# A macaron block with a state-space convolution: the convolution's rows turned by VectorE and gathered by DMA, the half chunk first in the last wave, and three bursts of small work cut into pieces

## The chip, the core and the metric

The kernel runs on one core of one Trainium2 chip. A core has TensorE (PE; its weight loads are listed apart as PEld), VectorE (DVE), ScalarE (ACT), GpSimd (POOL) and SyncE (SP), which here does nothing but issue DMAs, one after the other in the order of its queue. All five run their own instruction lists and meet at semaphores. The time is the device time of a whole launch in microseconds (us), the median of a few runs.

## The reference, cut to what matters

For 2048 rows of 1024 floats the block computes

```python
x = u                                            # (2, 1024, 1024) float32
x = x + 0.5 * ffn(layernorm(x))                  # silu(xn @ Wg) * (xn @ Wu) @ Wd, 4-bit weights
x = x + s4(layernorm(x))                         # causal convolution along the last axis, and D * u
x = x + 0.5 * ffn(layernorm(x))                  # the same weights again
```

Wg and Wu have shape (1024, 2752), Wd has (2752, 1024). A weight is `scales[g] * (w4 - (z4[g] + 1))` with one scale and zero point for each of 8 groups of 128 rows of Wg and Wu, and for each of 21.5 groups of Wd. The convolution in the middle runs along the 1024 columns of each row with one kernel K for all rows, so it is a product of the normalized rows with a Toeplitz matrix made from K.

## The kernel before, in words

**Jobs.** The 2048 rows are four blocks of 512 (`TB`), each four tiles of 128 rows (`t` = 0 to 3). A feed-forward pass over a block is a job. `JOBS` orders the eight: (block 0, first pass), (1, first), (0, second), (1, second), (2, first), (3, first), (2, second), (3, second). They are called job 0 to job 7 here. The work between two passes of a block (layer norm, convolution, layer norm) is hidden in the job that follows the block's first pass: block 0's in job 1, block 1's in job 2, block 2's in job 5, block 3's in job 6. These four are called the jobs with a convolution.

**Up and down.** `gate_up` runs 64 steps: 8 waves of column chunks, 8 groups of 128 contraction rows each. A chunk is 128 hidden columns, with a gate unit (even number) and an up unit (odd). The first five waves hold three chunks, that is six units, each in one PSUM bank of [128, 512]; the last three hold two, and the very last also the half chunk, unit 42, whose 64 gate and 64 up columns share a bank. In a step each unit gets two matmuls, one with the activations' low part `xTl` and one with the high part `xTh` (line 774). After each group the unit is multiplied in PSUM by a ratio of scales (`scaled`, lines 739 on ScalarE and 743 on VectorE), so that the unit's next matmul must wait for that. After the eighth group `gated` (lines 801, 804, 806, 808) makes the hidden chunk. `down` runs 44 steps in the same manner (line 849), four banks at a time. A step with six units has 12 matmuls, one with four 8, the last wave's 10.

**Weights.** For each step SP loads a tile of bytes (`load_bytes`, L700 and L707, six buffers) four steps ahead, and POOL casts it (L716, five buffers) three steps ahead. In job 0 the bytes are also made first: VectorE splits words (`split`, L590 to L594), POOL casts (L623), DMAs write and read them back.

**Order.** Side work is hung on steps: `at(up, s, f)` runs `f` when step `s` is written, at its middle for half numbers; `dn` is the same for `down`. A list scheduler then sets each engine's order; `in_order_of_writing` and `pinned` keep named engines in the order of the text. `in_pieces` lets a generator run one piece per step.

**The convolution before.** For each tile `norm` (`normalized`, L230) writes the normalized rows on VectorE, `swap` (`turn_whole`) has PE transpose them in eight 128x128 pieces into two PSUM banks (`turned`, L237), and ScalarE (L1260) and VectorE (L1258) copy a bank each to `st`. `convolve` then makes three sums on POOL (L1205, L1206 and the line after) and the products on PE (L1210) in two halves, which VectorE adds to `x` (L1240 to L1250). Counted in steps, with `late` = 33 in job 1 and 16 else, tile `t` is normalized at `late+8+4t`, turned at `late+10+4t` and multiplied at `late+12+4t`.

**Small work.** `scales_down` (one call at step 40 of job 0) turns the scales of Wd and makes their ratios in a handful of VectorE operations. `in_order` (one call at step 30 of job 2) checks on the chip that scales and group indices are as the fast way needs them; it ends with one matmul (L491) and a flag that is read at the very end.

**Buffers that the change shares.** `t4` tiles are [128, 1024] float32, ten buffers; `results_out` already turns the down product of each job with VectorE's 32x32 transposes (`turn_block`, L884) and sends it through DRAM (`rows_out`, L890: 32 partitions of 16 pieces of 512 bytes in one DMA).

Of the kernel before, what the change touches and what calls it, by code (L numbers as in the profile page):

```python
# [57 lines left out]
def macaron_s4_kernel(  # L58
# [320 lines left out]
    def inverse(inv, s, name):  # L379

        sq = t2(f"sq_{name}")[:, : s.shape[1]]
        nc.vector.tensor_tensor(sq, s, s, ALU.mult)
        nc.vector.scalar_tensor_tensor(inv, sq, 2.0**-60, s, ALU.is_lt, ALU.add)
        nc.vector.reciprocal(inv, inv)
# [47 lines left out]
    def scales_down(rows):  # L432
        ps = bank("ps_d")
        for i, row in enumerate(rows):
            for k in range(4):
                nc.tensor.transpose(
                    ps[:, bass.ts(4 * i + k, GD)], row[:GD, bass.ts(k, P)], ident[:GD, :GD]
                )
        n = NC * GD
        flat = s_dn.rearrange("p c g -> p (c g)")  # L440
        nc.vector.tensor_copy(flat, ps[:, :n])
        inv = t2("inv_d")[:, :n]
        inverse(inv, flat, "d")
# [3 lines left out]
        )  # L447
        nc.vector.tensor_scalar(
# [3 lines left out]
    def in_range(s, col):  # L452

        n = s.shape[1]
        sq = t2(f"rs_{col}")[:, :n]
        nc.vector.tensor_tensor(sq, s, s, ALU.mult)
        for k, (op, lim) in enumerate(((ALU.is_ge, 2.0**-60), (ALU.is_le, 2.0**60))):
            t = t2(f"rg_{col}_{k}")[:, :n]
            nc.vector.tensor_scalar(t, sq, lim, None, op)
            nc.vector.tensor_reduce(ok[:, col + k : col + k + 1], t, AX.X, ALU.min)  # L460

    def in_order():

        nc.gpsimd.memset(ok, 1.0)
        in_range(s_gu.rearrange("p u g -> p (u g)"), 0)
        in_range(s_dn.rearrange("p c g -> p (c g)"), 2)
# [11 lines left out]
        f = t4("ixf")[:32, : 3 * P].rearrange("p (i k) -> p i k", i=3)  # L478
        nc.vector.tensor_copy(f, raw)
        nc.vector.tensor_scalar(f, f, float(GD - 1), None, ALU.min)  # L480
        want = small.tile([32, 1], F32, tag="want", name="want")
        nc.vector.tensor_scalar(want, row_t[:32], float(GD - 1), None, ALU.min)
        nc.vector.tensor_scalar(f, f, want, None, ALU.is_equal)
        nc.vector.tensor_reduce(
            ok[:GK, 4:5], f[:GK, 0:2].rearrange("p i k -> p (i k)"), AX.X, ALU.min
        )
        nc.vector.tensor_reduce(ok[: full + 1, 5:6], f[: full + 1, 2], AX.X, ALU.min)
        all_ok = small.tile([P, 1], F32, tag="all_ok", name="all_ok")
        nc.vector.tensor_reduce(all_ok, ok[:, 0:6], AX.X, ALU.min)
        ps = bank("ps_ok")  # L490
        nc.tensor.matmul(ps[:1, :1], all_ok, ok[:, 6:7], start=True, stop=True)  # L491
        nc.vector.tensor_scalar(flag, ps[:1, :1], P - 0.5, None, ALU.is_lt)
# [252 lines left out]
    def gate_up(j, b, hooks):  # L745
        hi, lo = pieces[b]
        ps = {}
        for s, (wi, g) in enumerate(STEPS):
# [6 lines left out]
            if wi == len(WAVES) - 1:  # L755
                order.append((2 * WIDE, 2 * n))


            early = len(order) // 2
# [1085 lines left out]
```

## Time and profile before

| | us |
|---|---|
| median of 3 runs | 2079.88 (2078.57 to 2081.78) |
| the profiled execution, whole | 2081.12 |
| its span | 2079.2 |
| PE busy in the span | 2031.7 |
| DVE busy | 1670.2 |
| ACT busy | 1398.8 |
| POOL busy | 1352.6 |
| PE busy from 1571 to 1755 (up part of job 6, with a convolution) | 183.67 of 184 |
| PE busy from 1834 to 1989 (up part of job 7, without) | 155.00 of 155 |

The profiled execution took 1.92 us more than its span and 1.24 us more than the median. Busy times are unions, so overlapping matmuls count once. The granted clock of TensorE was 0.995 on average.

### The profile page before, as it was taken

How to read it: one execution, taken by the hardware profiler on the slowest of the kernel's cores; microseconds unless marked ns; L12 is line 12 of the kernel's file. 1: busy time of each engine (PE TensorE's matmuls, PEld its weight loads, DVE VectorE, ACT ScalarE, POOL GpSimd, SP SyncE). 2: the span in 40 equal slices, each digit the busy share in tenths (PEclk: the TensorE clock that was granted, in tenths of full speed). 3: DMA queues.
4: the chain of work that ended last, by engine and by line, in shares of the span. 5: the costliest groups of instructions: out<-in, count | busy, mean ns of one | idle time of the engine just before them, and what ended most of it. 6: DMA issues, size and time to landing. Idle time of an engine off the chain costs nothing.

```text
span 2079.2 us, 30011 instructions
## 1 busy us (share of the span) xinstructions
PE 2031.7 (98%) x9332; PEld 1388.2 (67%) x9332; DVE 1670.2 (80%) x2813; ACT 1398.8 (67%) x2185; POOL 1352.6 (65%) x1740
## 2 busy tenths in 40 slices
PE   6999999999999999999999999999999999999998
PEld 4555675676866768665776568667686676866576
DVE  8888878778789787797788877787877878777777
ACT  6677787645775477677777777664776647767775
POOL 5766668655875468755876568654696546975542
PEclk9999999999999999999999999999999999999999
DMA  4334323112621116511472116311164111661113
GB/s 143 118 91 143 109 82 83 35 55 51 164 81 40 51 45 158 177 34 35 105 177 95 32 43 156 101 40 48 36 152 113 40 48 33 149 183 50 34 35 101
DMA packets 278023, 180.38 MB, mean 87 GB/s; under 512 B 101253, under 2 KB 257774, under 8 KB 277854
## 3 DMA queue, kind: packets, MB, share of 16 engines
q1 hardware_dynamic: 276550, 175.96, 30.8%
q8 instruction: 76, 1.25, 0.3%
q10 hardware_dynamic: 1016, 1.82, 0.2%
q14 instruction: 93, 0.76, 0.1%
q0 software_dynamic: 288, 0.59, 0.1%
HBM read 119.13 MB, written 40.18 MB: 77 GB/s over the span
## 4 chain that ended last, share of the span: by engine, by line
PE 89%; DVE 6%; POOL 2%; DMA 1%; issue 1%; ACT 1%; SPq 0%; ACTq 0%; POOLq 0%; DVEq 0%
PE pg L774 55%; PE po L849 29%; PE pc L1210 3%; DVE pg L743 1%; PE pb L1210 1%; DMA b<-wq 1%; DVE po L743 1%; PE st L237 1%; DVE x L263 0%; POOL q L623 0%; DMA x<-in_L_attn_u_dram 0%; DVE hf L804 0%; POOL w_up L716 0%; DMA wq<-q 0%; DVE xn L230 0%
## 5 line engine op out<-in xcount | busy, mean ns | idle before, releaser
L739 ACT ACTIVATE pg<-pg,rat 128x512 f32<-128x512 f32 x1240 | 787.1, 660 | 418.2 <-PE pg L774 415.9
L743 DVE TENSOR_TENSOR pg<-pg,rat 128x512 f32<-128x512 f32 x1168 | 775.3, 692 | 162.3 <-PE pg L774 154.2
L774 PE MATMUL pg<-xTh,w_up 128*128 128x512 f32 x2752 | 851.4, 437 | 2.4 <-DVE pg L743 1.8
L774 PE MATMUL pg<-xTl,w_up 128*128 128x512 f16 x2752 | 717.6, 383 | 12.8 <-DVE pg L743 6.9
L716 POOL CAST w_up<-b 128x768 fp32r<-128x768 int8 (+2 forms) x490 | 375.4, 772 | 429.6 <-PE pg L774 323.0
L774 PEld LDWEIGHTS pg<-xTh,w_up 128*128 128x128 f32 x2752 | 520.6, 189 | 178.7 <-issue 14.3
L739 ACT ACTIVATE po<-po,ratd 128x512 f32<-128x512 f32 x660 | 432.0, 661 | 159.6 <-PE po L849 158.8
L849 PE MATMUL po<-hl,w_down 128*128 128x512 f32 x1344 | 528.8, 396 | 6.1 <-DVE po L743 5.3
L849 PE MATMUL po<-hh,w_down 128*128 128x512 f32 x1344 | 520.9, 391 | 0.0
L743 DVE TENSOR_TENSOR po<-po,ratd 128x512 f32<-128x512 f32 x620 | 429.1, 695 | 110.5 <-PE po L849 108.7
L774 PEld LDWEIGHTS <-w_up 128*128 128x128 bf16 x2752 | 226.6, 99 | 338.5 <-issue 159.5
L716 POOL CAST w_down<-bd 128x512 fp32r<-128x512 int8 x352 | 217.1, 620 | 149.7 <-PE po L849 87.8
L849 PEld LDWEIGHTS po<-hl,w_down 128*128 128x128 f32 x1344 | 251.7, 188 | 76.9 <-DVE po L743 15.6
L849 PEld LDWEIGHTS po<-hh,w_down 128*128 128x128 f32 x1344 | 253.0, 188 | 50.2
L808 POOL TENSOR_TENSOR hl<-hf,hh 128x512 fp32r<-128x512 f32 x168 | 219.4, 1306 | 8.0
L804 DVE SCALAR_TENSOR_TENSOR hf<-pg,rat,g 128x512 f32<-128x512 f32 x168 | 123.5, 747 | 42.3 <-ACT g L801 33.3
L806 POOL CAST hh<-hf 128x512 fp32r<-128x512 f32 x168 | 106.4, 634 | 65.8 <-DVE hf L804 33.0
L801 ACT ACTIVATE g<-pg,rat 128x512 f32<-128x512 f32 x168 | 110.8, 686 | 41.0 <-PE pg L774 26.2
L900 POOL TENSOR_TENSOR x<-x,yr 128x512 f32<-128x512 f32 x52 | 66.7, 1284 | 0.0
L289 POOL TENSOR_TENSOR lo<-x,hi 128x512 f16<-128x512 f32 x48 | 61.8, 1288 | 0.0
L189 DVE BATCH_NORM_STATS2 stats<-x 128x6 f32<-128x512 f32 x88 | 60.1, 682 | 0.0
L287 POOL TENSOR_TENSOR mid<-hi,top 128x512 bf16<-128x512 f32 x48 | 56.0, 1167 | 0.0
(219 smaller groups left out, 1106.0 us busy)
## 6 DMA issues: line engine op xcount, KB each, us to landing
b<-wq SPq DMA_DIRECT2D x319, 96.0 KB
bd<-wdq SPq DMA_DIRECT2D x336, 64.0 KB
x<-in_L_attn_u_dram SPq DMA_DIRECT2D x30, 512.0 KB
yz<-y SPq DMA_DIRECT2D x56, 256.0 KB
yr<-yz SPq DMA_DIRECT2D x56, 256.0 KB
b<-wq SPq DMA_DIRECT2D x128, 64.0 KB
xs<-x SPq DMA_DIRECT2D x16, 512.0 KB
x<-xs SPq DMA_DIRECT2D x16, 512.0 KB
```

The lines of the kernel that those rows point to most:

```text
L289: nc.gpsimd.tensor_tensor(lo[:, own], n[:, own], hi[:, own].bitcast(F32), ALU.subtract)
L716: nc.gpsimd.tensor_copy(t, b)
L739: nc.scalar.activation(dst, src, AF.Copy, scale=sc)
L743: nc.vector.tensor_tensor(dst, src, sc.to_broadcast(list(dst.shape)), ALU.mult)
L774: nc.tensor.matmul(p, weights, (lo, hi)[k][:, g, :], start=(g == 0 and not done), stop=(g == GK - 1 and done), skip_group_check=True,)
L801: nc.scalar.activation(g, pg, AF.Silu, scale=rat[:, 2 * f, GK - 1 :])
L804: nc.vector.scalar_tensor_tensor(hf, pu, last, g, ALU.mult, ALU.mult)
L806: nc.gpsimd.tensor_copy(hi, hf)
L808: nc.gpsimd.tensor_tensor(lo, hf, hi.bitcast(F32), ALU.subtract)
L849: nc.tensor.matmul(ps[c], w[:, bass.ts(c, P)], part, start=(f == 0 and k == 0), stop=(f == NF - 1), skip_group_check=True,)
L900: nc.gpsimd.tensor_tensor(part, part, rows_back.pop((a, t)), ALU.add)
L1210: nc.tensor.matmul(dst, lhsT, rhs, start=start, stop=stop, skip_group_check=True)
```

## The change

The normalized rows of a tile are no longer turned by PE. `rows_turned` normalizes them in two halves and then transposes 32x32 blocks in place, 256 columns at a time, six VectorE pieces on six half steps. `rows_stored` writes the tile to a DRAM tile (two of them, used in turn), and `columns_loaded` reads it back with four DMAs, one for each 32 partitions of `st`, 32x32 pieces of 32 floats (128 bytes) each, which completes the transposition. With `start_` = 36 and `gap` = 3.5 in job 1, 23 and 4 else, tile `t` starts at o = `start_ + gap*t`; the pieces lie at o to o+2.5, the store at o+4, the four loads at o+7, the product's halves at o+10 and o+11. The layer norms around it move with it.

The half chunk comes first instead of last in the last wave, and is now in its early group. In job 1 ScalarE takes every other scaling of each wave's first up unit for the whole job, not only up to step 32. `scales_down` is given in pieces from step 40 to 51.5, `in_order` in pieces over steps 36 to 59 of job 3, not at once in job 2. Some layer-norm pieces of other jobs move.

```diff
-    def inverse(inv, s, name):
+    def inverse_in_pieces(inv, s, name):
         sq = t2(f"sq_{name}")[:, : s.shape[1]]
         nc.vector.tensor_tensor(sq, s, s, ALU.mult)
+        yield
         nc.vector.scalar_tensor_tensor(inv, sq, 2.0**-60, s, ALU.is_lt, ALU.add)
+        yield
         nc.vector.reciprocal(inv, inv)
...
             if wi == len(WAVES) - 1:
-                order.append((2 * WIDE, 2 * n))
-            early = len(order) // 2
+                order.insert(0, (2 * WIDE, 2 * n))
+            early = (len(order) + 1) // 2
...
-                    if pos == 1:
-                        on_act = (j == 0 and g % 4 == 0) or (j == 1 and s < 32 and g % 2 == 0)
+                    if unit == 2 * fs[0] + 1:
+                        on_act = (j == 0 and g % 4 == 0) or (j == 1 and g % 2 == 0)
...
+    s_dram = [dpool.tile([P, HID], F32, tag=f"sz{i}", name=f"sz{i}") for i in range(2)]
...
-                    late, first = (33, 27) if j == 1 else (16, 15)
+                    first, start_, gap = (26, 36, 3.5) if j == 1 else (13, 23, 4)
...
-                    steps = [(up, late + 4 + i) for i in range(4)]
+                    steps = [(up, start_ + i - 4 if j != 1 else start_ - 2 + i / 2) for i in range(4)]
                     in_pieces(at, steps, lambda: deviations_in_pieces(pb, 2))
-                    def norm(t):
-                        s4n[t] = normalized(pb, t)
-                    def swap(t):
-                        s4x[t] = turn_whole(s4n.pop(t), f"st_{pb}_{t}")
+                    def rows_turned(t):
+                        m, r, _ = ln[pb, t]
+                        n = s4n[t] = t4(f"xn_{pb}_2_{t}")
+                        for half in range(2):
+                            own = bass.ts(half, 512)
+                            nc.vector.tensor_scalar(n[:, own], x[pb][t][:, own], m, r, ALU.subtract, ALU.mult)
+                            yield
+                        for i in range(4):
+                            own = n[:, bass.ts(i, 256)]
+                            nc.vector.transpose(own, own)
+                            yield
+                    def rows_stored(t):
+                        nc.sync.dma_start(s_dram[t % 2], s4n.pop(t))
+                    def columns_loaded(t):
+                        s4x[t] = s = t4(f"st_{pb}_{t}").rearrange("p (c t) -> p c t", c=NC)
+                        src = s_dram[t % 2].rearrange("(b i) (c a j) -> a i c b j", i=Q, a=NQ, j=Q)
+                        for q in range(NQ):
+                            dst = s[bass.ts(q, Q)].rearrange("p c (b j) -> p c b j", j=Q)
+                            nc.sync.dma_start(dst, src[q])
...
-                        at(up, late + 8 + 4 * t, lambda t=t: norm(t))
-                        at(up, late + 10 + 4 * t, lambda t=t: swap(t))
-                        at(up, late + 12 + 4 * t, lambda t=t: conv(t))
-                        at(up, late + 13 + 4 * t, lambda t=t: next(parts[t], None))
-                    steps = [(up, late + 15 + 4 * t + i) for t in range(NT) for i in range(2)]
+                        o = start_ + gap * t
+                        steps = [(up, o + i / 2) for i in range(6)]
+                        in_pieces(at, steps, lambda t=t: rows_turned(t))
+                        at(up, o + 4, pinned(lambda t=t: rows_stored(t), ET.SP))
+                        at(up, o + 7, pinned(lambda t=t: columns_loaded(t), ET.SP))
+                        at(up, o + 10, lambda t=t: conv(t))
+                        at(up, o + 11, lambda t=t: next(parts[t], None))
+                    steps = [(up, start_ + gap * t + 13 + i) for t in range(NT) for i in range(2)]
                     in_pieces(at, steps, lambda: moments_by_tile(pb, 3, halves=True))
...
-                at(up, 40, lambda: scales_down(rows.pop("down")))
+                steps = [(up, 40)] + [(up, 41.5 + 2 * i) for i in range(6)]
+                in_pieces(at, steps, lambda: scales_down(rows.pop("down")))
...
-            if j == 2:
-                at(up, 30, in_order)
+            if j == 3:
+                in_pieces(at, [(up, 36 + i) for i in range(24)], in_order)
...
-                        steps = [(up, s) for s in range(18, 27)]
+                        steps = [(up, s) for s in range(12, 21)]
                         in_pieces(at, steps, lambda: moments_by_tile(ab, 1, halves=True))
-                        steps = [(up, s) for s in range(28, 32)]
+                        steps = [(up, s) for s in range(21, 25)]
...
-                        d, where = ((23 + 4 * t + 2 * half, dn), (3 * t + half, dn))[min(j, 1)]
+                        d, where = (23 + 4 * t + 2 * half if j == 0 else (0.5, 6, 14, 20)[t] + half), dn
                         if j > 1:
-                            d, where = (50 if ak == 3 else 33) + 2 * t + half, up
+                            d, where = (54 if ak == 3 else 25) + 2 * t + half, up
```

## The prediction

> **What bounds the kernel now.** I read the page's busy times and chain first, then the stretches of the jobs, then PE's order of time where the change works, then VectorE's and SP's rows.
>
> ```profile
> PE 2031.7 (98%) x9332; PEld 1388.2 (67%) x9332; DVE 1670.2 (80%) x2813; ACT 1398.8 (67%) x2185; POOL 1352.6 (65%) x1740
> PE 89%; DVE 6%; POOL 2%; DMA 1%; issue 1%; ACT 1%; SPq 0%; ACTq 0%; POOLq 0%; DVEq 0%
> ...
> 1571.00:1755.00 184.00, 183.67 (x911) 120.66 (x911) 150.45 (x266) 112.65 (x177) 102.17 (x123) 1.00 0.18 53
> 1834.00:1989.00 155.00, 155.00 (x688) 93.26 (x688) 117.53 (x180) 110.23 (x173) 91.48 (x111) 1.00 0.25 75
> ```
>
> PE is busy 98% of the span and is 89% of the chain that ends last. The two stretches (columns: length, then busy time and count of PE, PEld, DVE, ACT, POOL, granted clock, DMA share, GB/s) are the up parts of job 6, with a convolution, and job 7, without: PE never stops in either, so the convolution's 29 us are PE's own work. What leaves PE there leaves the time, as long as nothing else comes to hold it up.
>
> PE's order of time (start, length, operation) shows what leaves:
>
> ```profile
> 1640.78 0.82 PE L774 MATMUL pg<-xTl,w_up 128*128 128x512 f16 x3
> 1641.44 1.04 PE L237 MATMUL st<-ident,xn 128*128 128x128 f32 x8
> 1642.31 0.81 PE L774 MATMUL pg<-xTl,w_up 128*128 128x512 f16 x3
> ```
>
> The next matmul starts 0.87 us after the first transpose, so a tile's eight transposes cost 0.87 us; the 1.04 overlaps.
>
> The other losses are a few waits in jobs 0, 1, 2 and 5 (in brackets: idle time before, and who ended it), and what follows two of them:
>
> ```profile
> 155.97 0.38 PE L774 MATMUL pg<-xTl,w_up 128*128 128x512 f16 x1 [2.14 <-DVE pg L743]
> 494.49 0.79 PE L849 MATMUL po<-hl,w_down 128*128 128x512 f32 x1 [1.95 <-DVE po L743]
> 672.86 0.19 PE L491 MATMUL ps_ok<-ok,all_ok 128*1 128x1 f32 x2 [0.46 <-DVE all_ok L489]
> ...
> 156.00:165.00 9.00, 8.70 (x30) 3.94 (x29) 7.37 (x12) 5.19 (x9) 4.20 (x6) 0.81 0.67 213
> 490.00:500.00 10.00, 7.72 (x25) 5.23 (x25) 9.31 (x13) 4.18 (x7) 8.63 (x12) 0.83 0.08 22
> ```
>
> After each 2 us wait the granted clock falls: 0.81 over 9 us and 0.83 over 10 us are both about 3.4 us at half speed (9 x 0.19 x 2; 10 x 0.17 x 2), which costs 1.7 us more.
>
> **The change, part by part.**
>
> *Transposes off PE.* Four jobs x 4 tiles x 0.87 = **-14.0 us**. The built order of the changed kernel has these 128 matmuls gone, so this part is real if nothing new stops PE. Sixteen ACT copies (585 ns) go too; ACT is at 67% and gains nothing by it.
>
> *VectorE's share.* Rows that price it (minimum/median/maximum in ns):
>
> ```profile
> L263 DVE TENSOR_SCALAR x<-x,mv,r x56: 528/539/1539, 253.7 to 1740.1; 128x512 f32<-128x512 f32 x56
> L230 DVE TENSOR_SCALAR xn<-x,mv,r x16: 793/803/1865, 414.1 to 1678.1; 128x1024 f32<-128x1024 f32 x16
> L884 DVE STREAM_TRANSPOSE y<-y x112: 402/433/436, 296.5 to 2038.7; 128x256 f32<-128x256 f32 x112
> L1258 DVE COPY st<-st x16: 676/682/692, 419.7 to 1696.2; 128x512 f32<-128x512 f32 x16
> ```
>
> Added per tile: 2 x 0.54 + 4 x 0.43 = 2.80 us. Removed: 0.80 + 0.68 = 1.48. Net +1.3 us, 5.3 us a job, in up parts where VectorE has 184 - 150 = 34 us free. Locally it is tight: an up step is 2.70 us (24 steps in 64.9 us at the start of job 6), VectorE scales three units of it at 0.63 us each when back to back (four took 2.52 us), and over the three steps of a tile's pieces it has 3 x 1.89 + 2.80 = 8.5 us to do in 8.1, with a free step behind. But this very load exists already: the down result's L884 transposes come two a step beside three scalings, and through them the chain is one unbroken PE piece:
>
> ```profile
> 838.18 107.63 PE pg L774 x479
> ```
>
> So I cost this at nothing in the forecast; the cover is the eight matmul slots (8 x 0.225 = 1.8 us) between a unit's last matmul of one step and its first of the next, of which the scaling takes 0.7. If the cover goes, the next scaling is late and PE waits in each tile (rival 1). Waits of 0.89 us in job 5 (at 1375 us) and 1.25 us in job 1 (at 415 to 425 us, for the st copies, sums and scalings) come from the long normalize and the copies that go: **-1.7**.
>
> *The way through DRAM.* The trace has no load in 128-byte pieces of this size. The nearest is the down result's store:
>
> ```profile
> L890 SPq DMA_DIRECT2D yz<-y x56: 318/721/1457, 306.2 to 2041.5; - x56
> SPq L700 <- POOL w_up L716: 761.4, 386, 6.8
> ```
>
> Four such DMAs in a row (at 848.5 us) hold SP 3.4 us, the last up to 1.46, and the byte load behind them 1.39 where 0.32 is its rule: once the queue is full, 512 pieces need 1.45 us, 2.8 ns a piece. By pieces a column load (1024) takes 2.9 us and a tile's four 11.6; by bytes (a load has half the 256 KB) 0.73 and 2.9. I take the pieces, the costlier. Behind the four on SP stand the byte loads of later steps. They have room: of SP's waits, 761 us are byte loads waiting for a free buffer. With 6 byte and 5 weight buffers load k may go when PE has done step k-11, and its cast may start when PE has done k-5, six steps or 16 us later; SP loses about 9 of them. Then the product: turned at o+2.5 steps (6.8 us), store landed about 3.5 us on, loads 11.6, landing 1.9 (the time to landing that the page has for POOL's stores): 23.8 us, against 27 us at step o+10. In job 1 the steps after 40 take 1.8 us; by the same sum its loads of tiles 1 and 2 are 1 to 2 us late. POOL's three sums wait in its queue, casts behind them, but casts run three steps ahead. I take **+2.5 us** for job 1 and jitter together (0 by bytes, up to 6).
>
> Here the Trainium skill speaks against the change: "DMA: Bandwidth & Descriptors", Rules for kernel authors, wants a turning DMA to be the hardware's transpose and not a rearranged pattern, and puts 19x between them. The trace's DMA transposes of a 256 KB tile hold SP 1.25 us (L294); two of them for float32, times 19, would be 47 us a tile, 30 more than the 17 us (four steps and a product of 6.2) that a tile has, and 16 x 30 us on the sum. I follow L890: pieces of 128 bytes are no single elements, and a scattered store at 2.8 ns a piece is in this trace.
>
> *scales_down in pieces.* The 2.14 us wait in job 0 stands between its operations of 1.18, 1.39 and 1.19 us (L382, L383, L384), bunched with `split`. Spread over 12 steps, each meets the slack alone. Worth 2.14 plus 1.7 of clock. By the skill ("TensorE: Matmul & The Clock Gate", table of goals) only idle gaps over about 3 us lower the clock, so by the rule 2.1; the trace has the fall after 2.14 and 1.95, and I go by it: up to 3.8. Some may return as a wait for the weights that job 0 is making, so **-3.0** (0 to -3.9).
>
> *Half chunk first, job 1's scalings and layer norm.* At job 0's end PE waits 1.35 us for a scaling behind the half chunk's split on VectorE (L823, L825); the half chunk now ends six matmuls (1.35 us) sooner: **-0.7** (+0.5 to -1.5). At job 1's end there are waits of 0.33, 1.95, 0.55 and 0.34 us behind deviations, L818 and L263, and 1.7 of clock, 4.9 together. The deviations now end half a step sooner, normalizing starts half a step later and is spread over 21 down steps, L818 comes sooner, and sixteen scalings of 0.69 us go to ACT. But the last product comes about a step later, so **-2.5** (+1 to -4.5).
>
> *The check.* Job 2's 0.46 wait and a 0.54 wait at 649 us among its L459 pieces go; in job 3 its pieces are single and its matmul stands a step behind its operand: **-0.9**. The other layer-norm pieces move within up parts where VectorE has a fifth free, and the block that they read is loaded from step 6: nothing.
>
> Sum: -14.0 - 1.7 + 2.5 - 3.0 - 0.7 - 2.5 - 0.9 = **-20.3**. From the profiled execution 2081.12 - 20.3 = 2060.8; that run stood 1.24 over the median, so the median becomes 2079.88 - 20.3 = **2059.6**.
>
> **The rivals.** *1, VectorE becomes the bound around the tiles.* For: 8.5 us in 8.1. L263 reaches 1.5 us where it meets other work. Against: the unbroken stretch at 838. At 0.6 us in each of 16 tiles, +10: 2070 (2066 to 2075).
>
> *2, the waits of jobs 0 and 1 only move.* For: VectorE is 85% busy there. Then -14.0 - 1.7 - 0.9 + 2.5 = -14.1: 2066.
>
> *3, slower: SP's queue is overrun by the column loads.* A tile has 17 us; other loads take about 2 of them. From (17 - 2)/4096 = 3.7 ns a piece lateness piles up from tile to tile, in the convolution jobs; all of the gain is gone at 20/16 = 1.25 us a tile, 4.0 ns. At 6 ns a tile needs 26.6, 9.6 too many; only the tiles after the first of each job are late, 12 x 9.6 = 115: about 2175. For: 2.8 is not far from 3.7, and the kind is not in the trace. Against: pieces carry a quarter of L890's bytes.
>
> That the change doesn't do what it says is excluded for the transposes by the built order.
>
> **How the numbers follow.** The forecast 0.68 (2053 to 2066), rival 1 0.16, rival 2 0.07, rival 3 0.06, something between that ends at no change 0.03. Faster by over 0.2% (4.2 us, about what a measurement can tell): 0.68 + 0.16 + 0.07 = 0.91; within 0.2%: 0.03; slower: 0.06. The range reaches from all gains at their bounds (2053.5) into rival 1 (2070.5).
>
> **What would show it.** Right: L237 keeps only job 0's 32 transposes; job 6's up part is about 180.5 us with PE busy throughout; the clock stays at 1.00 at 150 to 165 and at 480 to 500 us; 128-byte DMAs hold SP under 3 us. Wrong: PE waits before L1210 for a POOL sum or a DMA (rival 3), before L774 for L743 within the pieces of each tile (rival 1), or a clock of 0.8 again at either place (rival 2).

## The result, and the profile after

| | median, us | runs |
|---|---|---|
| before | 2080.83 | 2078.57 to 2082.32 |
| after | 2065.81 | 2064.28 to 2067.67 |

Each was timed four times here; before's first three are those of the table further up. The ratio is 0.9929, with a 95% interval from 0.9912 to 0.9946: 15.0 us faster (11 to 18). The forecast was 2059.6, in a range from 2053.5 to 2070.5. The profiled execution has a span of 2062.2 us where before had 2079.2.

The profile after, first the busy times and then the chain by engine:

```profile
PE 2011.6 (98%) x9204; PEld 1370.9 (66%) x9204; DVE 1666.7 (81%) x2861; ACT 1397.5 (68%) x2185; POOL 1349.8 (65%) x1740
PE 88%; DVE 4%; POOL 2%; DMA 2%; issue 1%; ACT 1%; SPq 0%; ACTq 0%; POOLq 0%; DVEq 0%
```

PE has 128 matmuls fewer and is busy for 20.1 us less: 14.0 are the transposes, and most of the rest is the clock, which fell in four windows fewer (further down). It still bounds everything. The stretches that answer to those of before (length, busy time and count of PE, PEld, DVE, ACT, POOL, granted clock, DMA share, GB/s): the up parts of job 6 and job 7, and the two places where the clock fell:

```profile
1557.00:1740.00 183.00, 180.96 (x881) 117.11 (x880) 152.08 (x281) 110.35 (x174) 100.04 (x123) 1.00 0.30 76
1818.00:1973.00 155.00, 155.00 (x690) 93.40 (x689) 118.00 (x180) 110.64 (x174) 91.43 (x111) 1.00 0.25 76
150.00:165.00 15.00, 14.48 (x63) 7.31 (x61) 13.20 (x23) 12.26 (x21) 10.44 (x12) 1.00 0.51 151
480.00:500.00 20.00, 19.31 (x82) 13.67 (x81) 17.46 (x32) 14.47 (x23) 16.09 (x22) 1.00 0.11 32
```

Both places have the full clock now. But job 6, where PE was without a gap before, has 2.04 us of gaps, and is only 1.3 us shorter (from its first matmul of up to its first of down, 183.1 instead of 184.4), although 3.5 us of transposes are gone. PE's list of waits (what waited, for what: total us, times, longest us) names the new one, and PE's order of time shows the first of the six (in brackets: idle before, and what ended it; `pc` and `pb` are the two PSUM banks of a tile's products):

```profile
PE pb L1232 <- POOL sums L1227: 5.7, 6, 1.7
```

```profile
653.35 1.47 PE L1232 MATMUL pc<-near,st 128*128 128x256 f32 x8
654.65 0.39 PE L1232 MATMUL pc<-after,st 128*128 128x128 f32 x2
654.88 0.39 PE L1232 MATMUL pc<-ahead,st 128*128 128x128 f32 x2
656.94 0.49 PE L1232 MATMUL pb<-near,sums 128*128 128x128 f32 x2 [1.68 <-POOL sums L1227]
```

The products from `st` run, so the columns are there; only the product from `sums` waits. POOL's order of time at that moment says why:

```profile
653.43 0.60 POOL L827 CAST hh<-hf 128x512 fp32r<-128x512 f32 x1
654.12 1.26 POOL L829 TENSOR_TENSOR hl<-hf,hh 128x512 fp32r<-128x512 f32 x1
655.33 0.61 POOL L827 CAST hh<-hf 128x512 fp32r<-128x512 f32 x1
655.90 0.99 POOL L1227 TENSOR_TENSOR sums<-st 128x384 f32<-128x384 f32 x1
```

The first sum, for which PE waits, stands behind the splitting of the wave's three hidden chunks (three `hh` and two `hl`), which comes at the end of each wave. The new steps put a tile's product at the second step of a wave (step 33), where this splitting is under way. PE waits 1.68 us for the first tile and 0.22 us for the third, in each of jobs 2, 5 and 6.

The DMA that finishes the turning is cheap (count, then minimum/median/maximum ns on SP):

```profile
L1564 SPq DMA_DIRECT2D st<-sz x64: 562/675/1885, 407.3 to 1679.5; - x64
L1553 DVE STREAM_TRANSPOSE xn<-xn x64: 390/432/445, 399.5 to 1669.3; 128x256 f32<-128x256 f32 x64
```

1024 pieces of 128 bytes hold SP 0.68 us, and no product waits for `st`. VectorE's part did no harm in these jobs: in job 5 PE is one piece of the chain through the steps in which the rows of the first tiles are turned.

```profile
1295.06 86.47 PE pg L795 x384
```

Taken apart by job (time from the first matmul of one job to that of the next, less the same in before; the last column is the span):

| us | job 0 | 1 | 2 | 3 | 4 | 5 | 6 | 7 | span |
|---|---|---|---|---|---|---|---|---|---|
| after | -2.6 | -6.4 | -3.3 | +0.4 | -0.3 | -2.3 | -1.5 | -0.9 | -17.0 |

Part of jobs 0 and 1 is the clock: the profiled execution of before had half clock in five windows of 3.41 us (1.7 us lost in each; two near 80 us, one each at 156, 364 and 494), that of after in one, near 80 us. Over the executions on record the mean granted clock is 0.9961 for before (47 of them, timed beside the experiments) and 0.9975 for after (4). As an estimate from these, 0.0014 of 2080 us, some 3 of the 15 us are the clock.

### The profile page after: what moved, and what is told of

Read it like the earlier page. It is cut to its first block, busy times and chain, and to the rows that moved or that the text cites. A ratio compares the mean times of both kernels' runs of the same rounds, so it can differ in the third digit from the quotient of the medians.

```text
span 2062.2 us, 29944 instructions
## 1 busy us (share of the span) xinstructions
PE 2011.6 (98%) x9204; PEld 1370.9 (66%) x9204; DVE 1666.7 (81%) x2861; ACT 1397.5 (68%) x2185; POOL 1349.8 (65%) x1740
## 4 chain that ended last, share of the span: by engine, by line
PE 88%; DVE 4%; POOL 2%; DMA 2%; issue 1%; ACT 1%; SPq 0%; ACTq 0%; POOLq 0%; DVEq 0%
PE pg L795 54%; PE po L870 29%; PE pc L1232 3%; PE pb L1232 1%; DVE pg L764 1%; DMA b<-wq 1%; POOL hh L827 0%; DMA bd<-wdq 0%; POOL hl L829 0%; ACT pg L760 0%; POOL w_up L737 0%; POOL q L644 0%; DVE po L764 0%; ACT g L822 0%; DMA x<-in_L_attn_u_dram 0%
## 5 line engine op out<-in xcount | busy, mean ns | idle before, releaser
L764 DVE TENSOR_TENSOR pg<-pg,rat 128x512 f32<-128x512 f32 x1152 | 764.7, 691 | 144.7 <-PE pg L795 136.9
L870 PEld LDWEIGHTS po<-hl,w_down 128*128 128x128 f32 x1344 | 251.7, 188 | 69.5 <-DVE po L764 11.3
```

The costliest lines, as they stand in the source:

```text
L764: nc.vector.tensor_tensor(dst, src, sc.to_broadcast(list(dst.shape)), ALU.mult)
L870: nc.tensor.matmul(ps[c], w[:, bass.ts(c, P)], part, start=(f == 0 and k == 0), stop=(f == NF - 1), skip_group_check=True,)
```

## The experiments

Each kernel was timed beside the kernel before. An interval is some 3 us to either side, so effects below that are read from the traces.

| kernel | median, us | ratio to before (95%) |
|---|---|---|
| e1, products two steps later | 2058.54 | 0.9904 (0.9889 to 0.9919) |
| e10, sums alone earlier | 2062.59 | 0.9919 (0.9905 to 0.9932) |
| e2, transposes on TensorE, all else changed | 2070.39 | 0.9959 (0.9946 to 0.9973) |
| e3, convolution's part alone | 2075.27 | 0.9984 (0.9977 to 0.9991) |
| e4, scales of Wd in one burst | 2068.20 | 0.9946 (0.9932 to 0.9960) |
| e5, half chunk last | 2067.81 | 0.9939 (0.9926 to 0.9953) |
| e6, job 1's normalizing back | 2064.76 | 0.9922 (0.9909 to 0.9936) |
| e11, job 1's rule of scalings back | 2067.10 | 0.9938 (0.9924 to 0.9951) |
| e7, column loads twice, same place | 2143.90 | 1.0308 (1.0294 to 1.0322) |
| e7b, twice, other place | 2111.49 | 1.0149 (1.0134 to 1.0165) |
| e7c, twice, PE's order held | 2105.34 | 1.0117 (1.0101 to 1.0134) |
| e9, e1 and two edits | 2055.84 | 0.9883 (0.9868 to 0.9898) |

### e1: the products two steps later

```diff
-                        at(up, o + 10, lambda t=t: conv(t))
-                        at(up, o + 11, lambda t=t: next(parts[t], None))
+                        on = 10 if j == 1 else 12
+                        at(up, o + on, lambda t=t: conv(t))
+                        at(up, o + on + 1, lambda t=t: next(parts[t], None))
...
```

The layer norm's moments and deviations behind the products are two steps later as well, the deviations now at half steps.

> The changed kernel, with the Toeplitz products of every tile two steps later in jobs 2, 5 and 6 (steps start + 12 and 13 after the tile's first piece instead of 10 and 11), and the moments and deviations behind them two steps later; job 1 as it was. Theory T (the sums of POOL come late): the changed kernel's TensorE waits 1.68 us ahead of the first tile's pb product and 0.22 us ahead of the third tile's in each of these three jobs, because POOL's sums stand behind the hh and hl pieces at the wave boundary; two steps later (about 5 us) they are ready, so 3 x 1.9 = 5.7 us come back, about 2060 us if the changed kernel is at 2065.8. Rival V (VectorE is too crowded, so whatever is moved is late somewhere else): the additions behind the products come late and the wait turns up at the next matmul that needs a bank, no more than 1 us gained. Rival C (the loads of the columns are late): gains as much as T does, so this run alone does not tell T from C.

Measured: 2058.54, 7.3 us below the changed kernel. No product waits for a sum any more. PE's order at the same tile, and the up part of job 6:

```profile
660.20 0.39 PE L1232 MATMUL pc<-after,st 128*128 128x128 f32 x2
660.42 0.39 PE L1232 MATMUL pc<-ahead,st 128*128 128x128 f32 x2
660.65 0.39 PE L1232 MATMUL pb<-near,sums 128*128 128x128 f32 x2
```

```profile
1551.00:1731.00 180.00, 179.82 (x880) 116.69 (x879) 151.57 (x281) 110.46 (x174) 101.10 (x123) 1.00 0.30 77
```

Job 6's up part takes 180.3 us: the 180.5 that the prediction had named. Each of jobs 2, 5 and 6 is 2.8 us shorter than in the changed kernel, though its listed waits were 1.9. At the first tile the next matmul from `w_up` starts 2.38 us after the two from `ahead` in the changed kernel (654.88 to 657.26) and 0.45 us in e1 (660.42 to 660.87): 1.93 us for a listed wait of 1.68. By the same count the third tile costs 0.53 us for a listed 0.22, and the last 0.3 us of a job come behind the tiles, from step 49 on. Rival V is out, since VectorE's additions came two steps later as well and no new wait for them is listed.

### e10: only the sums earlier

```diff
+        yield
...
-                        at(up, o + 10, lambda t=t: conv(t))
+                        at(up, o + (10 if j == 1 else 8.5), lambda t=t: summed(t))
+                        at(up, o + 10, lambda t=t: next(parts[t]))
```

The `yield` stands in `convolve`, behind the third sum.

> The changed kernel, with only POOL's three sums of a tile written 1.5 steps ahead of the tile's products in jobs 2, 5 and 6 (at start + 8.5 instead of 10); the products and all else stay. In POOL's queue the first tile's sums then stand ahead of one hh and one hl piece (about 1.9 us together in the trace of the changed kernel). Theory T (the sums wait for POOL's queue): the waits of 1.68 us shrink to nothing, 4 to 5.7 us gained over the three jobs. Rival C (the columns land late, so POOL waits for the load): the sums cannot start sooner, the hh and hl pieces behind them are held up as well, no gain or a loss of 1 to 3 us.

Measured: 2062.59, 3.2 below the changed kernel. The built order has moved the three sums ahead of the wave's last `hh` (0.61 us) and last `hl`; the three long waits are 1.12 us instead of 1.68, the short ones are gone:

```profile
PE pb L1233 <- POOL sums L1227: 3.4, 3, 1.1
```

Less than expected, since two `hh` and two `hl` still stand ahead. But with the same loads at the same time, and all that moved being POOL's order, the wait shrank. In the changed kernel the first tile's four loads are out of SP's hands at 642.6 us, 10.7 us ahead of its products:

```profile
639.83 2.81 SPq L1564 DMA_DIRECT2D st<-sz  x4
```

These products read `st` and ran 3.6 us ahead of the one from `sums`. The columns are not what is late (rival C); the place in POOL's queue is.

### e2 and e3: the two halves of the change

e2 is the changed kernel with the convolution's old lines back, and nothing else undone; e3 is the kernel before with the new lines alone. In short, as e2 changes it (and e3 the other way round, from before):

```diff
-                        in_pieces(at, steps, lambda t=t: rows_turned(t))
-                        at(up, o + 4, pinned(lambda t=t: rows_stored(t), ET.SP))
-                        at(up, o + 7, pinned(lambda t=t: columns_loaded(t), ET.SP))
-                        at(up, o + 10, lambda t=t: conv(t))
+                        at(up, late + 8 + 4 * t, lambda t=t: norm(t))
+                        at(up, late + 10 + 4 * t, lambda t=t: swap(t))
+                        at(up, late + 12 + 4 * t, lambda t=t: conv(t))
...
-                            d, where = (54 if ak == 3 else 25) + 2 * t + half, up
+                            d, where = (50 if ak == 3 else 25) + 2 * t + half, up
```

> The changed kernel with the convolution's part put back as it was before: transposes on TensorE, copies by ScalarE and VectorE, the old steps of the products. All other parts stay (half chunk first, job 1's scaling rule and normalizing, the scales of w_down and the check in pieces, the layer norms of jobs 3 and 4 earlier). Theory T: these other parts gain what the two traces show outside the tiles: about 2.6 us by the end of job 0, some 3 us at the end of job 1, about 0.9 us of the check's waits in job 2, less 0.6 us given back in jobs 3 and 4: 5 to 7 us below the kernel before, so about 2074 to 2076 us, and the two falls of the clock (at 156 us and at 494 us in the kernel before) are gone here too. Rival L (the missing clock falls are luck of one execution, or come from the quieter TensorE queue of the new convolution): no more than 3 us below the kernel before.

> The kernel before with the convolution's part of the change alone: rows turned by VectorE, stored and gathered by DMA, products, moments and deviations at their new steps. Theory T: 14 us of transposes and the waits at the turned tiles come off TensorE, 5 to 6 us are given back as waits for POOL's sums in jobs 2, 5 and 6: 8 to 10 us below the kernel before, about 2071 to 2073 us. The two parts add up: this gain and that of the other parts make the 15 us. Rival V (VectorE takes the place): less than 6 us, with TensorE waiting for VectorE's scaled products in the tiles' stretches. Rival L (nearly all of the gain is the convolution's): 12 us or more.

By job, against before:

| us | job 0 | 1 | 2 | 3 | 4 | 5 | 6 | 7 | span |
|---|---|---|---|---|---|---|---|---|---|
| e2 | -4.6 | -4.8 | -2.3 | +0.6 | -0.3 | -1.0 | -0.4 | -0.3 | -13.2 |
| e3 | -2.8 | -3.4 | +1.6 | 0.0 | -0.1 | -1.9 | -1.0 | +0.2 | -7.3 |
| e1 | -2.1 | -6.8 | -6.1 | +0.4 | -0.3 | -5.1 | -4.3 | -0.1 | -24.4 |

By medians e2 gains 8.9 us and e3 only 4.05 (both ratios are clear of 1); e2's is more than expected, e3's far less. The convolution's part, with 14 us of transposes in it, is the smaller half of the gain. e3's gain lies in rival V's range (less than 6 us), but the sign that V named is not there: PE waits 7.0 us for VectorE's scaled products of the up parts, and 8.7 in before. In jobs 2, 5 and 6 the changed kernel is only 1.0 to 1.3 us a job better than e2, and e1 3.8 to 4.1. So turned rows are worth 3.8 to 4.1 us a job where nothing takes them back, and the sums took 2.8 of it.

In job 2 e3 is even slower than before. It has a wait of 1.18 us for the sums, another of 1.95 us for the third tile's, and half the clock for 3.41 us behind that, so that 1.7 us of job 2 are the clock. The check still ran there in one burst, at step 30.

```profile
659.20 0.49 PE L1211 MATMUL pb<-near,sums 128*128 128x128 f32 x2 [1.18 <-POOL sums L1206]
690.00:710.00 20.00, 17.70 (x91) 13.15 (x89) 12.28 (x21) 6.95 (x11) 10.45 (x15) 0.91 0.24 42
```

In job 1 the part alone won nothing: its up part took 192.4 us, where before had 193.0 with one clock window in it (191.3 without). The part needs the new rule of scalings there, which e11 shows.

### e4, e5, e6, e11: one small part undone

e4: the six pieces of `scales_down` in one call at step 40.

```diff
-                in_pieces(at, steps, lambda: scales_down(rows.pop("down")))
+                at(up, 40, lambda: [None for _ in scales_down(rows.pop("down"))])
```

> The changed kernel with the scales of w_down worked out at step 40 of job 0 in one burst, as before the change. Theory T: VectorE is held in one stretch at the start of wave 5, its scaled product is late there and TensorE waits 2.1 us at about 152 us instead of 0.43: 1.7 us lost for certain, and 1.7 us more in those executions in which the clock falls to 0.5 for 3.4 us behind it (it did in the kernel before, and did not in the kernel with the convolution's part alone, with the same wait). So 1.7 to 3.4 us slower than the changed kernel. Rival L (the pieces only spread the loss over the waits of 0.36 to 0.57 us at 186 to 191 us): those shrink by as much, less than 0.7 us lost.

Measured: 2.4 us above the changed kernel by medians. The wait is back:

```profile
154.86 0.38 PE L795 MATMUL pg<-xTl,w_up 128*128 128x512 f16 x1 [2.17 <-DVE pg L764]
150.00:165.00 15.00, 12.22 (x51) 5.91 (x48) 13.65 (x21) 10.35 (x18) 8.66 (x11) 1.00 0.59 186
```

Wave 5 takes 2.35 us more, and 1.2 us are left of it at the start of down, because the waits at 175 to 192 us are 0.7 us shorter (1.1 instead of 1.85 in all) and the rest closes up as well. No clock was lost at this place this time. So the pieces are worth about 1.2 us; both theories had a part of it. The figure is one trace against one: in kernels whose job 0 is the same, waves 6 and 7 together differ from the changed kernel by -0.9 to +0.6 us. And over e4's five executions the mean granted clock is 0.9956, where the changed kernel has 0.9975, so the clock has a share in the 2.4 us.

e5: half chunk last.

```diff
-                order.insert(0, (2 * WIDE, 2 * n))
-            early = (len(order) + 1) // 2
+                order.append((2 * WIDE, 2 * n))
+            early = len(order) // 2
...
-                    if unit == 2 * fs[0] + 1:
+                    if pos == 1:
```

> The changed kernel with the half chunk last in the last wave again, with the rule of the copies that belongs to it. The prediction gave half first 0.7 us in job 0. Theory T, from the traces: the waits at the end of job 0 and the start of its down part (1.4, 0.9 and 1.8 us) stand in all kernels with half first, where before had 1.35 and 1.16; so half first gains nothing in job 0, and undoing it gains 0 to 1.5 us there, while in jobs 1 to 7 nothing moves by more than 0.1 us each. Rival H (half first is what took the waits off the end of job 1 and the other jobs' seams): 0.3 us or more lost in each of jobs 1 to 7, 2 us or more in all.

Measured: 2.0 us above by medians, 3.7 by span. Half first costs about 1 us in job 0 (1.1 from wave 3 to the end, 1.5 in e9, which has the half chunk last in job 0 alone; kernels with the same job 0 differ there by up to 0.8 us, clock windows taken off at 1.7) and gains 0.5 to 0.8 in each of jobs 2 to 7: rival H for most of the run. In the second half of job 0's down part before, e3, e5 and e9, which have the half chunk last there, are each 0.6 us shorter than the changed kernel. No wait is listed for the gain in jobs 2 to 7. With the half chunk last, every second step of the last wave has one start-to-start interval of 0.31 instead of 0.22 us, and four of the first matmuls of down are stretched in the same way, where the changed kernel has one. The last wave of job 3, e5 and then the changed kernel:

```profile
965.18:983.26 18.08, 18.08 (x82) 10.76 (x80) 12.85 (x20) 12.66 (x21) 8.91 (x12) 1.00 0.11 31
```

```profile
964.43:982.22 17.79, 17.79 (x82) 10.76 (x80) 13.12 (x20) 12.88 (x21) 8.89 (x12) 1.00 0.11 31
```

PE is busy to the last digit in both, and one takes 0.29 us more.

e6 has job 1's normalizing back at its old steps, e11 job 1's old rule of scalings.

```diff
-                        d, where = (... else (0.5, 6, 14, 20)[t] + half), dn       # e6
+                        d, where = (... else 3 * t + half), dn
...
-                        on_act = (j == 0 and g % 4 == 0) or (j == 1 and g % 2 == 0)            # e11
+                        on_act = (j == 0 and g % 4 == 0) or (j == 1 and s < 32 and g % 2 == 0)
```

> The changed kernel with the normalizing halves of job 1's down part back at the steps 3t and 3t+1 (instead of 0.5, 6, 14, 20 and one later). Theory T: VectorE gets two 512-column halves early in the first down steps, its share of the scaled products is late and the wait of nearly 2 us at about 490 us returns, with smaller ones after it: 1.5 to 2.5 us lost, and 1.7 us more where the clock falls behind it. Rival S (it was the scaling rule of job 1, with every second group of the second unit on ScalarE past step 32, that took them away): less than 0.5 us lost, the waits at 488 to 513 us stay at 0.2 to 0.5 us each.

> The changed kernel with job 1's rule of the scaled copies as it was: ScalarE takes every second group of the first chunk's second unit up to step 32 only, no longer to the end. Undoing the normalizing steps alone left the end of job 1 at rest, so theory S: it is this rule that took the waits away; VectorE has two scaled products more in each group of waves 4 to 7, the wait of 1.4 to 2 us at about 490 us returns with 0.3 to 0.6 us behind it: 1.5 to 2.5 us lost at the end of job 1, 1.7 us more if the clock falls. Rival: neither the rule nor the steps alone, but both together (with one of them in place VectorE keeps up): less than 0.5 us lost here as well. Second rival: the waits came from the check and burst work that stood elsewhere; nothing changes here either, and the end of job 1 is decided by the convolution's new steps.

Measured: e6 the same as the changed kernel (2064.76 against 2065.81), e11 1.3 us above. In neither did the wait of nearly 2 us at about 490 us come back; where both are undone, with the half chunk last as well (e3), it is 1.41 us. So either one is enough for job 1's end as it is in the changed kernel, and theory T of e6 fell. What the rule does is in the up part (e11, then the changed kernel):

```profile
291.06:485.36 194.30, 190.31 (x905) 119.12 (x905) 155.29 (x309) 120.46 (x193) 120.59 (x182) 0.99 0.32 80
```

```profile
292.91:483.31 190.40, 187.83 (x906) 118.63 (x905) 146.65 (x295) 128.83 (x209) 120.64 (x182) 1.00 0.32 82
```

The rule takes 8.6 us of scalings off VectorE, and the up part is 3.9 us shorter, 2.2 without the clock window that e11 had. Without the rule the turned rows lose in job 1 (192.6 without the clock window, against e2's 191.67). That VectorE sets the pace there, as rival 1 had it, is argued from the load that the rule moves and not shown: of the waits of up's matmuls that e11 has behind 415 us and the changed kernel has not, one is for POOL's cast of weights (0.44 us), one for ScalarE (0.23) and one for VectorE (0.46). With it they gain 1.3 us (190.4 against e2's 191.67), not 3.5: two waits are there that e2 does not have.

```profile
PE s_k L1159 <- POOL s_rest L1153: 0.9, 1, 0.9
PE s_t L1186 <- DMA s_rows<-k_dram: 0.4, 1, 0.4
```

They belong to the making of K, which has its last steps in this job; one of them is POOL again.

### e7, e7b, e7c: the loads of columns twice

e7c also holds PE's matmuls in the order of the text.

```diff
-                            nc.sync.dma_start(dst, src[q])
+                            for _ in range(2):                         # e7
+                                nc.sync.dma_start(dst, src[q])
...
                             nc.sync.dma_start(dst, src[q])             # e7b and e7c
+                            dst = spare.rearrange("p (c b j) -> p c b j", c=NC, j=Q)[bass.ts(q, Q)]
+                            nc.sync.dma_start(dst, src[q])
```

> The changed kernel with every load of a tile's columns issued twice into the same place, so 8 such loads a tile instead of 4, 64 more in the run, each of 1024 pieces of 128 bytes. Theory T (a load goes by its bytes, about 0.68 us of its queue in the trace of the changed kernel, and nothing on the critical path waits for it): SyncE is held some 2.7 us longer a tile, 3 steps ahead of the products; 0 to 2 us more in all, no wait of TensorE for st. Rival C (the loads are the price of the change, at 2.8 ns a piece as the prediction had it): 2.9 us more for each added load, 11.6 us a tile, the columns land after the step of the products: 40 us or more on top.

> The changed kernel with every load of columns issued a second time, now into a DRAM buffer that nobody reads, right behind the load itself: the same 1024 pieces of 128 bytes and 128 KB each, but no load waits for the one before it to land, as it had to where both went into the same place (there SyncE was held up to 19 us for a tile's eight loads, and 78 us were lost). Theory T (the transfers are cheap, it was the waiting for landings in SyncE's queue that cost): SyncE is held 4 x 0.7 = 2.8 us longer a tile, the columns still land ahead of their products, at most 3 us more over 16 tiles. Rival C (the pieces themselves are the cost, 2.9 us a load or more at the far end): 40 us or more, with TensorE waiting for st as before.

> The doubled loads of columns once more (second copy into a DRAM buffer that nobody reads), now with TensorE's matmuls of the up parts of jobs 1, 2, 5 and 6, the tiles' products among them, held in the order in which they are written. In the two doubled kernels before, the planner that orders the instructions at build time had reckoned the columns later and put the products of several tiles behind other matmuls, close together or a wave later, so their 30 and 78 us were those of another order, not of the transfers. Theory T (1024 pieces of 128 bytes hold SyncE 0.68 us, and the columns land well ahead of the products): with the products at the changed kernel's steps the 64 added loads cost 0 to 6 us over the changed kernel, 2065 to 2072 us, and no product waits for st. Rival C (the pieces are the cost, the columns land late): the products wait for st and for the sums, 40 us or more over the changed kernel, 2105 us or more.

All three missed theory T by far: 78, 46 and 40 us above the changed kernel. In e7 the second load must wait until the first has landed, and twelve such loads, with six other DMAs between them, take SP from 671 to 690 us; there four products did wait for `st`, 18.7 us in all and 11.3 the longest. In e7b and e7c no load waits for another; e7c's SP in order of time:

```profile
651.62 0.63 SPq L1566 DMA_DIRECT2D st<-sz  x1
652.31 0.67 SPq L1568 DMA_DIRECT2D spare<-sz  x1
```

Eight in a row take 5.8 us, 0.63 to 0.74 us each, and no product waits for `st`. On SP each costs what a single one cost. The loss is again in the sums (e7c's waits, and POOL's order at the first tile of job 2):

```profile
PE pb L1234 <- POOL sums L1229: 26.7, 8, 3.9
```

```profile
667.38 1.26 POOL L830 TENSOR_TENSOR hl<-hf,hh 128x512 fp32r<-128x512 f32 x1
668.58 0.82 POOL L737 CAST w_up<-b 128x768 fp32r<-128x768 int8 x1
669.36 0.99 POOL L1229 TENSOR_TENSOR sums<-st 128x384 f32<-128x384 f32 x1
```

The list scheduler has set the sums behind the last `hl` and a cast, presumably because it reckons the columns later; PE's order was held in e7c, POOL's was not. The waits are 21.0 us more than in the changed kernel, and in the convolution jobs the clock was at half speed for 37.5 us (eleven times 3.41), 18.8 us lost, where the changed kernel has no such window. Together 40 of the 45 us between the two spans. So rival C is out as a price of transfers, and a load that is planned later is still dear, through POOL's order. A run with POOL's order held as well was not made, so that the loads alone would be free is argued, not shown.

### e9: e1, and two more edits

```diff
-                order.insert(0, (2 * WIDE, 2 * n))
+                order.insert(0 if j else len(order), (2 * WIDE, 2 * n))
...
-                        steps = [(up, s) for s in range(12, 21)]
+                        steps = [(up, s) for s in range(18, 27)]
```

> The changed kernel with three edits, each at a place of its own in the run: the products two steps later in jobs 2, 5 and 6 (as in the run before, which gave 7 us there), the next block's moments, deviations and normalizing of jobs 3 and 4 back at their old steps, and the half chunk last in job 0 alone (first in all other jobs). Theory T: the first edit gives its 7 us again; the second takes away the two waits of 0.23 and 0.47 us in each of jobs 3 and 4 and leaves the old ones of 0.15 to 0.28 us, 0.2 to 0.7 us gained over the two jobs; the third gives 0.5 us in job 0, while the 0.5 us that half first was worth in each of jobs 2 to 7 stay. In all 1 us below the first edit alone, about 2057.5 us. Rival: the waits in jobs 3 and 4 only move to the old steps, and job 0's waits are set by the writing of the weights: no gain beyond the first edit's.

Measured: 2055.84 us, 24 us below before (ratio 0.9883), the fastest of all, 10 below the changed kernel. From e1 it can't be told apart by times (0.9868 to 0.9898 against 0.9889 to 0.9919). By the traces the half chunk last in job 0 alone gains 1.5 us there against the changed kernel, as wanted. The old steps in jobs 3 and 4 lose 0.6 us over the two (waits of 0.81 and 0.92 us in place of 0.70): the rival was right, and the new steps should stay.

## Why the prediction was right, and which of its terms were not

The result lies in the range, 6.2 us above the forecast of 2059.6. But the sum of -20.3 was made of terms that were off in both directions, and that their errors nearly cancel is luck. Rival 2's 2066 meets the measured time only by chance: its cause was that the waits of jobs 0 and 1 move, and the one large loss lies in jobs 2, 5 and 6.

*Transposes off PE, -14.0.* The mechanism and the size were right: job 6 takes 180.3 us, with 180.5 foretold, once the sums are out of the way (e1), and jobs 2, 5 and 6 gain 3.8 to 4.1 each. In job 1 they gave 1.3, with 1.3 us of new waits (`s_k`, `s_t`) that the sum did not have.

*"POOL's three sums wait in its queue, casts behind them, but casts run three steps ahead", costed at nothing.* This is the step that failed. The sentence looked at who stands behind the sums, and not at what stands ahead of them at the new step: the splitting of a wave's hidden chunks. It cost 2.8 us in each of three jobs, 8.4 in all (7.3 by medians). The warning that the prediction gave for rival 3, "PE waits before L1210 for a POOL sum", came true without rival 3.

*The waits behind the long normalizing and the copies, -1.7.* Right: of the 1.25 us at 415 to 425 us in job 1, 0.17 is left in the changed kernel, and in e1 job 5 gains 0.8 us more than job 6.

*The way through DRAM, 2.9 us for a column load.* Mis-sized by four: 0.68 us, 0.66 ns a piece and not 2.8. The price taken from the down result's store did not carry over, and the other end, by bytes (0.73), was right. No product waited for `st`, so the +2.5 for late columns was not spent. Rival 3's break-even of 4.0 ns is far off. The 19x that the Trainium skill puts on rearranged patterns ("DMA: Bandwidth & Descriptors", Rules for kernel authors) had been set aside, and rightly here: a tile's four loads in pieces of 128 bytes hold SP 2.8 us (e7c's eight in a row 5.8), not the 47 us that the prediction worked out from it.

*VectorE's share at nothing.* Right in jobs 2, 5 and 6, not in job 1, where without the rule of the scalings all of the gain and more is gone (e3, e11), though not shown to VectorE's account alone.

*scales_down, -3.0.* The wait of 2.17 us goes, 1.2 us of it net. The 1.7 us of clock that the sum added are lost in some executions only: they were in before's trace, and not at this place in e3's or e4's, both with the wait. What decides that stands in the last section.

*Half chunk first, -0.7 in job 0.* Wrong in place: it cost about 1 us in job 0, and gained about 3.5 us in jobs 2 to 7, where the sum had nothing.

*Job 1's end, -2.5.* The down part's first half is 3.8 us shorter than in the profiled before, 1.7 of it clock. The change has two cures for it, either of which is enough (e6, e11).

*The check, -0.9.* It goes; job 2 gains 2.3 us even with transposes on TensorE (e2), the half chunk's 0.5 among them. Job 3, to which its pieces went, is 0.4 us longer.

By the two halves: the convolution's part stood at -13.2 in the sum (-14.0, -1.7, +2.5) and was worth 4.6 (after against e2; 3.8 by the profiled spans), the rest stood at -7.1 and was worth 8.9 (e2 against before). Of these 8.9 some 3 are the clock, an estimate like that for the changed kernel, since e2's mean granted clock is 0.9976.

## What to carry to other kernels

When a product is moved to another step, look at every engine that feeds it, at what stands ahead of it in that engine's queue at the new step; a step or two to the side, where nothing else falls due, was worth half as much again as the whole change. A change that takes work off TensorE by giving it to VectorE pays only where VectorE has room in that very stage, so move the load there in the same edit, as the rule of job 1 does. And double a cost only where the order can't change with it, or the answer is that of another order.

## What the runs showed of the hardware

*The clock.* In every trace half speed comes in whole windows of 3.41 us, one, two or (once, in e7) four together, and all windows of an execution lie on one fixed grid. Before's begin at 77.73, 156.24, 364.45 and 494.16 us, the last three 23, 84 and 122 windows behind the first. The grid stands elsewhere in each execution. What decides is how long PE is busy within one window of it. In the fourteen traces, from some 20 us on to the last matmuls, 34 windows at full speed had PE busy for less than 1.49 us, and half speed followed all 34. It followed two of the six with 1.49 to 1.64 us, and nine of the 8304 busier ones.

Before and e3 have the same wait of 2.14 us. In before it lies within one window; in e3 an edge of the grid cuts it, and the clock stays (two windows in a row of before, then of e3; PE's busy time follows the length, and the clock is the column before the DMA share):

```profile
152.83:156.24 3.41, 1.27 (x7) 0.62 (x5) 3.41 (x5) 1.62 (x3) 2.87 (x4) 1.00 0.29 95
156.24:159.65 3.41, 3.41 (x9) 1.41 (x8) 2.93 (x5) 1.32 (x2) 0.00 (x0) 0.50 0.53 155
```

```profile
154.25 0.38 PE L774 MATMUL pg<-xTl,w_up 128*128 128x512 f16 x1 [2.14 <-DVE pg L743]
152.48:155.89 3.41, 1.51 (x6) 0.68 (x5) 3.41 (x5) 0.87 (x2) 1.57 (x2) 1.00 0.38 112
155.89:159.31 3.42, 2.94 (x12) 1.35 (x13) 2.87 (x6) 2.02 (x5) 1.42 (x3) 1.00 0.72 238
```

The nine that do not fit all lie at 356 to 365 us, in job 1, and hold at least fifteen of sixteen matmuls of only 8 columns, for K (before's):

```profile
362.26 1.95 PE L1056 MATMUL s_sums<-s_vc,s_sq 128*128 128x8 f32 x16 [0.57 <-DVE s_vc L1034]
361.04:364.45 3.41, 2.84 (x21) 2.10 (x20) 2.76 (x7) 0.82 (x2) 2.95 (x4) 1.00 0.20 54
364.45:367.87 3.42, 3.42 (x9) 2.17 (x8) 0.03 (x1) 1.82 (x3) 3.42 (x9) 0.50 0.02 2
```

In four of the other five traces an edge of the grid cuts the sixteen. If they are left out of PE's busy time, the nine windows have 0.30 to 0.36 of their length and fit; that the clock counts so is inferred, and since e2 has all sixteen in one window with 0.39 and stays at full speed, they may count for a little.

From the bounds of 1.49 and 1.64 us follows, as an estimate, what a single wait does in full work: under 1.8 us it does not bring the clock down (none of the seventeen waits of about 1.7 us for sums did), over 3.8 us it always does, wherever the grid stands (e7c's six of 3.8 to 3.9 us all did), and between them it is the grid's place, which no edit sets. The Trainium skill's figure of about 3 us ("TensorE: Matmul & The Clock Gate", table of goals) is then no edge in these runs, where waits of 2.14 us and of 1.95 (with one of 0.33 just ahead) brought the clock down in before. A saving that counts on the clock behind a wait of some 2 us should be counted as a chance.

*A wait listed is not all that it costs.* A wait listed at 1.68 us put the next matmul 1.93 us later. And the half chunk's 0.5 us a job is in no list at all: only the times at which the same matmul starts in two kernels show it.
